# Idle rounds between the dependent steps of a closing that runs beside the scans of the next image

## The chip, the cores and the metric

The kernel runs on one core of one Trainium2 chip. The metric is the device time of one execution in microseconds (us); a lower number is better. Names of engines are those of the profile: PE is TensorE (PEld its weight loads), DVE is VectorE, ACT is ScalarE, POOL is GpSimd, SP is SyncE, which here only issues DMAs.

## The reference

Four images of 4096 tokens and 128 channels go through two layers, all in 32-bit floats.

```python
# layer 0: group norm, three selective scans (forward, backward, sliced order), out-projection, residual
x = x + conv(gn(x))
#   per order: silu(causal conv of the in-projection); delta = softplus(...)
#   h = h * exp(delta * A) + (delta * u) * B ;  y = sum_n h * C + D * u ;  y *= silu(z)
# layer 1: t are the tokens of x
t = t + attn(ln(t))
#   q = ring of cosines of (ln(t) + theta), 16 heads of 8;  softmax(q q^T / sqrt(8)) q
#   x1 = ln(x + ctx @ w_comb.T + b_comb)
#   z = cos(x1[:, :8]) * cos(ry);  out = ln(x1 + relu(z @ w1.T + b1) @ w2.T + b2)
t = t + experts(ln(t))
#   64 experts choose 8 tokens each by softmax(ln(t) @ gate.T); gelu network; scatter-add
```

## The kernel before

The work is issued in an order that the Python program writes out by hand (`tc.manual_schedule()`). Each engine takes its instructions in that order. The program mixes several streams of work. Every stream is a generator, and each `yield` in it ends one step.

**The main stream** is the attention loop of one image, `Attention.loop(b, beside)`. It has 1024 rounds (4 head groups, 8 blocks of 512 queries, 32 blocks of 128 keys). A round issues on PE the score matmuls of the next round (L917) and the value matmuls of this one (L931), and on ACT two exponentials of 128x1024 (`e<-s`, L922). At the end of a round `beside(i)` is called, which gives steps to the other streams. The four loops follow each other; before the rounds of a loop, SP issues the 16 loads of its `qT` and `v` (L896, L897).

**The scans** (`Scans.of_image`, the Pace `following`) of the next image run beside the loops of images 0, 1 and 2, 384 scan steps for an image. A scan step is two generator steps. In its first half it issues the loads of a later step (`delta`, `du`, on SP), the exponential of the next step (`exp`, ACT, L522) and, when its number modulo 4 (`turn`) is 1 or 2, the `y` sums of finished steps (PE, L570). In its second half it issues on DVE the scan (L538, 2.35 us) and two products (L529, L543, 1.2 us each); at `turn` 2 also `out` (L586), which reads `y` out of PSUM on DVE. Beside the loops the scans are paced so that they end near round 860.

**One PSUM bank** of the eight is left for everything beside the loop (`Bank(..., 1)`). `y` holds it from `turn` 1 to `turn` 2. Others ask for it with `bank.take`, which yields `PE` first; `beside` lets such a step go only when the bank is free and, as long as scans are left, only in a *slot*: a call of `beside` in which the scans issued an exponential but no sums (`turn` 3 and 0).

**The closing** (`Attention.after(b)`, the Pace `last`) is what remains of an image after its loop. It runs beside the next image's loop, at the front of it, one step in a round. For images 0 and 1 this is beside the scans of images 2 and 3 (loops 1 and 2); for image 2 it is beside the last loop, where no scans are left. Its parts:

- `shares()`: load the softmax totals (SP, L1001), take the reciprocal (DVE, L1003), store it (POOL, L1004).
- `first(g)` for 8 groups of 512 tokens: loads; `cT*part` (DVE, L1018); two halves of `co` (take, PE L1025; add on DVE L1028); a norm; store.
- `cosines()`: DVE and one sine on ACT.
- `second(g)` for 8 groups: transpose of z (`zt`), four `h` (PE L1059, evacuated on DVE L1062), four `fo` (PE L1069, added on DVE L1073), two norms with stores, transpose `xT` (L1090), `lg` (L1099).

`norm` makes statistics on DVE, a reciprocal root on POOL (`rstd_of`), yields, and scales on DVE (L831). `flow(pieces, 2, apart)` runs two groups at once, one step of each in turn; only one group at a time may hold the tile `h`, and the other one waits for it by yielding (`hidden`).

**The opening** of the next image (`opening(b + 1)`) starts when the scans of that image are done and the closing is done. What is left of closing or opening after round 1023 runs with no attention beside it:

```python
other = last if not last.done else opens if left == 0.0 else None
if other is None:
    return
slot = left == 0.0 or "exp" in scans.did and "sum" not in scans.did
if other.then is not PE or not bank.free:
    other.run(1.0)
    slot = slot and left > 0.0
if slot and other.then is PE and bank.free:
    other.run(1.0)
```

Of the kernel before, what the change touches and what calls it, by code (L numbers as in the profile page):

```python
# [669 lines left out]
class Attention:  # L670
# [3 lines left out]
    def __init__(self, tc, ctx, w, gate, cols, ident, bank, dram, t1, w_out, sums, sz, x):  # L674
        nc = self.nc = tc.nc
        gate_w, gate_b = gate
        self.tc, self.cols, self.ident, self.bank, self.dram, self.t1 = tc, cols, ident, bank, dram, t1
        self.w_out, self.sums, self.sz, self.x = w_out, sums, sz, x
        const = ctx.enter_context(tc.tile_pool(name="a_const", bufs=1))
        self.half_pi = column(nc, const, math.pi / 2.0, "a_half_pi")  # L680

        def rows(name, n):
            t = const.tile([P, n], F32, name=f"bc_{name}")
            nc.scalar.dma_start(out=t, in_=w[name].partition_broadcast(P))
            return t

        self.theta = rows("rx_theta", D)
        self.bc = {k: rows(k, C) for k in ("b_comb", "b2", "g1", "beta1", "g2", "beta2")}
        self.b1 = const.tile([P, 4], F32, name="b1")
        nc.scalar.dma_start(out=self.b1, in_=w["b1"].rearrange("(f p) -> p f", p=P))  # L690
        self.cos_ry = const.tile([D, 3], F32, name="cos_ry")
        nc.scalar.dma_start(out=self.cos_ry[:, 0:1], in_=w["ry_theta"].unsqueeze(1))
        cosine(nc, self.cos_ry[:, 2:3], self.cos_ry[:, 0:1], self.cos_ry[:, 1:2], self.half_pi)
        self.w_comb = const.tile([P, C], F32, name="w_comb")
        self.w1 = const.tile([D, FFN], F32, name="w1")
        self.w2 = const.tile([P, 4, C], F32, name="w2")

        self.mask = const.tile([P, 4], F32, name="mask")
        self.gate = const.tile([P, E], F32, name="gate")
        self.gate_b = const.tile([2 * E, 1], F32, name="gate_b")  # L700
        for k in range(2):
            nc.scalar.dma_start(out=self.gate_b[k * E : (k + 1) * E], in_=gate_b.unsqueeze(1))
        with tc.tile_pool(name="a_load", bufs=1) as load, tc.tile_pool(
            name="a_load_ps", bufs=2, space=PSUM
        ) as load_ps:
            raw = load.tile([P, C], F32, name="raw_comb")
            nc.sync.dma_start(out=raw, in_=w["w_comb"])
            ps = load_ps.tile([P, 512], F32, tag="ps", name="ps_comb")
            nc.tensor.transpose(ps[:, :C], raw, ident)
            nc.vector.tensor_copy(self.w_comb, ps[:, :C])  # L710
            raw = load.tile([P, 4, D], F32, name="raw_w1")
            nc.sync.dma_start(out=raw, in_=w["w1"].rearrange("(f p) d -> p f d", p=P))
            ps = load_ps.tile([P, 512], F32, tag="ps", name="ps_w1")
            for f in range(4):
                nc.tensor.transpose(ps[:D, f * P : (f + 1) * P], raw[:, f, :], ident)
            nc.vector.tensor_copy(self.w1, ps[:D])
            raw = load.tile([P, FFN], F32, name="raw_w2")
            nc.sync.dma_start(out=raw, in_=w["w2"])
            ps = load_ps.tile([P, 512], F32, tag="ps", name="ps_w2")
            for f in range(4):  # L720
                nc.tensor.transpose(ps[:, f * P : (f + 1) * P], raw[:, f * P : (f + 1) * P], ident)
            nc.vector.tensor_copy(self.w2.rearrange("p f c -> p (f c)"), ps)
            raw = load.tile([4, 4, 4, D], F32, name="raw_mask")
            nc.gpsimd.memset(raw, 0.0)
            nc.gpsimd.affine_select(
                out=raw, in_=raw, compare_op=ALU.not_equal, fill=1.0,
                base=0, pattern=[[0, 4], [-1, 4], [0, D]], channel_multiplier=1,
            )
            ps = load_ps.tile([P, 512], F32, tag="ps", name="ps_mask")
            nc.tensor.transpose(ps[:, :4], raw.rearrange("j i k d -> j (i k d)"), ident[:4, :4])  # L730
            nc.vector.tensor_copy(self.mask, ps[:, :4])
            raw = load.tile([E, C], F32, name="raw_gate")
            nc.scalar.dma_start(out=raw, in_=gate_w)
            ps = load_ps.tile([P, 512], F32, tag="ps", name="ps_gate")
            nc.tensor.transpose(ps[:, :E], raw, ident[:E, :E])
            nc.vector.tensor_copy(self.gate, ps[:, :E])
        self.small = ctx.enter_context(tc.tile_pool(name="a_small", bufs=2))
        self.u, self.q, self.v, self.context, self.total, self.t2 = {}, {}, {}, {}, {}, {}
        self.xn, self.logits, self.angled, self.whole, self.closed = {}, {}, {}, {}, {}

    def begin(self, loop):

# [25 lines left out]
    def tokens(self, b, g, angles):  # L768
# [47 lines left out]
        self.angled[b] += 1  # L816
        yield

    def norm(self, out, src, name):

        nc = self.nc
        stats = self.small.tile([P, 4, 6], F32, tag="ln_stats", name=f"st_{name}")
        mv = self.small.tile([P, 4, 2], F32, tag="ln_mv", name=f"mv_{name}")
        rstd = self.small.tile([P, 4], F32, tag="ln_rstd", name=f"rs_{name}")
        for i in range(4):
            nc.vector.bn_stats(stats[:, i, :], src[:, i, :])
            nc.vector.bn_aggr(mv[:, i, :], stats[:, i, :])
        rstd_of(nc, rstd, mv[:, :, 1], *self.cols)
        yield
        for i in range(4):  # L830
            nc.vector.tensor_scalar(  # L831
                out[:, i, :], src[:, i, :], mv[:, i, 0:1], rstd[:, i : i + 1], ALU.subtract, ALU.mult
            )
# [140 lines left out]
    def after(self, b, gs=range(L // QB), to=None):  # L974
# [21 lines left out]
        def shares():  # L996
            def rows(t):
                return t.rearrange("q h t -> (q h t)").rearrange("(p t) -> p t", p=P)

            t = self.piece([P, len(gs) * H * QB // P], "p0", name=f"sum_{b}_{gs[0]}")  # L1000
            nc.sync.dma_start(out=t, in_=rows(self.total[b][blocks]))  # L1001
            yield
            nc.vector.reciprocal(t, t)  # L1003
            nc.gpsimd.dma_start(out=rows(share), in_=t)  # L1004
            yield

        def first(g):
            cut = slice(g * 4, g * 4 + 4)
# [6 lines left out]
                out=part, in_=share[g - gs[0]].unsqueeze(1).to_broadcast([H, D, 512])  # L1015
            )
            yield
            nc.vector.tensor_mul(cT, cT, part)  # L1018
            yield
            yield  # L1020
            for half in range(2):
                ps = yield from self.bank.take(f"co_{b}_{g}_{half}")
                for k in range(2):
                    at = slice((2 * half + k) * P, (2 * half + k + 1) * P)
                    nc.tensor.matmul(ps[:, k * C : (k + 1) * C], cT[:, at], self.w_comb, start=True, stop=True)  # L1025
                yield
                u_h = flat(u[:, 2 * half : 2 * half + 2, :])
                nc.vector.tensor_add(u_h, u_h, ps[:, : 2 * C])  # L1028
                self.bank.leave()
# [8 lines left out]
        def second(g):  # L1038
# [11 lines left out]
            self.bank.leave()  # L1050
            yield
            yield
            while self.hidden == max(1, self.n - 1):
                yield
            self.hidden += 1
            h = self.one.tile([P, 4, 512], F32, tag="h", bufs=max(1, self.n - 1), name=f"h_{b}_{g}")
            for f in range(4):
                ps = yield from self.bank.take(f"h_{b}_{g}_{f}")
                nc.tensor.matmul(ps, self.w1[:, f * P : (f + 1) * P], zT, start=True, stop=True)  # L1059
                yield  # L1060
                if self.n == 2:
                    nc.vector.tensor_scalar(h[:, f, :], ps, self.b1[:, f : f + 1], 0.0, ALU.add, ALU.max)  # L1062
                else:
                    nc.scalar.activation(h[:, f, :], ps, AF.Relu, bias=self.b1[:, f : f + 1])
                self.bank.leave()
            for k in range(4):
                ps = yield from self.bank.take(f"fo_{b}_{g}_{k}")
                for f in range(4):
# [16 lines left out]
            nc.gpsimd.dma_start(out=self.xn[b][:, cut, :], in_=u)  # L1085
            yield
            yield
            ps = yield from self.bank.take(f"xT_{b}_{g}")
            for k in range(4):
                nc.tensor.transpose(ps[:, k * P : (k + 1) * P], u[:, k, :], self.ident)  # L1090
# [3 lines left out]
            self.bank.leave()  # L1094
            yield
            yield
            ps = yield from self.bank.take(f"lg_{b}_{g}")
            rows = slice(E, 2 * E) if to else slice(0, E)
            nc.tensor.matmul(ps[rows], self.gate, xT, start=True, stop=True)  # L1099
# [304 lines left out]
def tile_kernel(tc, ctx, x, in_proj_w, dirs, out_proj_w, attn, gate, weight1, weight2, out):  # L1404
# [47 lines left out]
    with tc.manual_schedule():  # L1452
        last = Pace()
        n = 3 * NC * NB
        for b in range(nb - 1):
            opens = Pace(block.opening(b + 1))

            def beside(i):

                left = 2.1 * (n + 1 - scans.steps.get(b + 1, 0))  # L1460
                scans.did.clear()
                following.run(min(1.3, max(0.5, left / max(1, 860 - i))))
                other = last if not last.done else opens if left == 0.0 else None
# [14 lines left out]
                following.run(0.5 if ready else 1.0)  # L1478
            last = Pace(block.after(b))
        following.rest()  # L1480

    scanning.close()
    experts = Experts(tc, ctx, ident, weight1, weight2, block, nb)
# [65 lines left out]
```

## Time and profile before

| what | value |
|---|---|
| median of 3 runs | 12901.4 us (12900.43 to 12902.03) |
| profiled execution, its own time | 12908.77 us |
| span of the profile | 12907.1 us |
| PE, ACT, DVE, POOL busy | 94%, 83%, 68%, 24% of the span |
| loop 1 (image 1, beside it closing of image 0, scans of image 2) | from 4991.9 us, 2597 us for its 1024 rounds |
| loop 2 (image 2, beside it closing of image 1, scans of image 3) | from 7593.0 us, 2580 us |

The profile is one execution. Busy time of PE is modelled, so a PE that is busy is not always a PE at its peak; a stretch in which it is idle is real. A round number in this document is counted in the trace: two exponentials `e` (L922) make one round, and the first of a loop is its round 0.

### The profile page before, as it was taken

The numbers are of one execution on the slowest core, as the hardware profiler recorded it, in microseconds if no ns is written. First come the engines' busy times: TensorE is split into PE (matmuls) and PEld (weight loads), VectorE is DVE, ScalarE is ACT, GpSimd is POOL, SyncE is SP. The second block draws the span as 40 slices with busy tenths as digits, with TensorE's granted clock in tenths as the row PEclk, the third lists the DMA queues.
The fourth block names the chain that finished last, engine by engine and source line by source line (L and its number), as shares of the span: only waits on it lengthen the run. The fifth ranks groups of instructions, "written<-read, shape, count | busy, mean of one in ns | idle before, by whom it ended". The sixth has DMA issues, their size and how long they took to land.

```text
span 12907.1 us, 215600 instructions
## 1 busy us (share of the span) xinstructions
PE 12125.7 (94%) x85447; PEld 3883.9 (30%) x85447; DVE 8730.9 (68%) x8912; ACT 10718.9 (83%) x10812; POOL 3129.4 (24%) x4007
## 2 busy tenths in 40 slices
PE   7888887599999999999999999999999999999996
PEld 3333333122222222333322222333222223333323
DVE  7999998788888877888887778888874211101112
ACT  5676766499999988999999889999998888888882
POOL 2324342232223222223232223232321000000000
PEclk9898988799999999999999999999999999999997
DMA  5666666555555455554554555545543100000004
GB/s 163 198 190 183 186 183 193 138 134 139 139 135 138 121 151 143 134 132 127 127 131 121 146 143 135 133 125 131 127 122 97 54 20 13 22 17 22 13 22 169
DMA packets 775661, 1553.29 MB, mean 120 GB/s; under 512 B 205198, under 2 KB 392134, under 8 KB 774390
## 3 DMA queue, kind: packets, MB, share of 16 engines
q1 hardware_dynamic: 590686, 1127.02, 33.7%
q0 software_dynamic: 142464, 302.77, 7.6%
q10 hardware_dynamic: 41496, 109.71, 3.3%
q8 instruction: 669, 10.96, 0.4%
q14 instruction: 346, 2.83, 0.1%
HBM read 1230.07 MB, written 308.81 MB: 119 GB/s over the span
## 4 chain that ended last, share of the span: by engine, by line
PE 80%; DVE 7%; ACT 5%; issue 4%; DMA 3%; SPq 1%; POOL 0%; ACTq 0%; DVEq 0%; POOLq 0%
PE s L917 36%; PE acc L931 29%; PE y L570 4%; PE cv L378 3%; DVE h L538 3%; PE sp L436 2%; PE fo L1069 1%; ACT e L922 1%; PE h L1059 1%; PE xd L392 1%; DVE dB L529 1%; DMA du<-d_du 1%; DMA w<-in_L_ffn_weight_dram 0%; DMA d_y<-o 0%; ACT e L424 0%
## 5 line engine op out<-in xcount | busy, mean ns | idle before, releaser
L922 ACT ACTIVATE e<-s 128x1024 f32<-128x1024 f32 x8192 | 7905.1, 1027 | 1107.0 <-PE s L917 940.4
L917 PE MATMUL s<-qm,qT 32*128 32x512 f32 x32768 | 5437.2, 642 | 112.5 <-DMA qT<-d_q 58.0
L931 PE MATMUL acc<-e,v 128*32 128x512 f32 x32768 | 4386.6, 607 | 24.4 <-ACT av L940 21.9
L917 PEld LDWEIGHTS s<-qm,qT 32*128 32x128 f32 x32768 | 1792.8, 183 | 3199.9 <-PE s L917 1408.6
L540 POOL COPY ends<-h 128x1 f32<-128x1 f32 x1152 | 1375.3, 1196 | 2875.1 <-DVE h L538 2866.0
L931 PEld LDWEIGHTS acc<-e,v 128*32 128x32 f32 x32768 | 646.9, 108 | 3162.8 <-issue 3021.4
L538 DVE TENSOR_TENSOR_SCAN h<-delta,ends,du 128x1024 f32<-128x1024 f32 x576 | 1351.6, 2347 | 196.6 <-ACT delta L522 162.2
L538 DVE TENSOR_TENSOR_SCAN h<-dA,ends,dB 128x1024 f32<-128x1024 f32 x576 | 1351.4, 2346 | 128.0 <-ACT dA L522 115.4
L529 DVE TENSOR_TENSOR dB<-du,B 128x1024 f32<-128x1024 f32 x768 | 929.6, 1210 | 657.1 <-PE y L570 595.0
L522 ACT ACTIVATE dA<-delta,A 128x1024 f32<-128x1024 f32 x768 | 888.0, 1156 | 147.3 <-DMA delta<-d_delta 146.3
L522 ACT ACTIVATE delta<-delta,A 128x1024 f32<-128x1024 f32 x768 | 887.1, 1155 | 137.6 <-PE y L570 127.8
L543 DVE TENSOR_TENSOR du<-h,C 128x1024 f32<-128x1024 f32 x768 | 936.5, 1219 | 0.1
L543 DVE TENSOR_TENSOR dB<-h,C 128x1024 f32<-128x1024 f32 x768 | 936.4, 1219 | 0.0
L529 DVE TENSOR_TENSOR du<-du,B 128x1024 f32<-128x1024 f32 x768 | 922.2, 1201 | 0.4 <-DMA B<-d_bc 0.3
L946 POOL DMA_DIRECT2D d_ctx<-av x512 | 259.9, 517 | 1248.2 <-ACT av L940 1242.7
L378 PE MATMUL cv<-xn,conv 128*128 128x512 f32 x1024 | 490.5, 632 | 33.0 <-DVE xn L313 17.3
L570 PE MATMUL y<-du,sel 128*32 128x256 f32 x6144 | 483.9, 387 | 17.3 <-DVE du L543 17.3
L570 PE MATMUL y<-dB,sel 128*32 128x256 f32 x6144 | 486.8, 389 | 4.3 <-DVE dB L543 3.4
L538 DVE TENSOR_TENSOR_SCAN h<-delta,du 128x1024 f32<-128x1024 f32 x192 | 438.7, 2285 | 45.8 <-ACT delta L522 37.8
L599 POOL DMA_DIRECT2D d_y<-o x512 | 328.5, 671 | 562.9 <-DVE o L586 430.8
L538 DVE TENSOR_TENSOR_SCAN h<-dA,dB 128x1024 f32<-128x1024 f32 x192 | 438.6, 2284 | 36.8 <-ACT dA L522 35.9
L564 POOL DMA_DIRECT2D d_du<-x_delta x272 | 154.4, 568 | 1132.2 <-DVE x_delta L563 1069.1
(255 smaller groups left out, 7643.6 us busy)
## 6 DMA issues: line engine op xcount, KB each, us to landing
delta<-d_delta SPq DMA_DIRECT2D x768, 512.0 KB
du<-d_du SPq DMA_DIRECT2D x576, 512.0 KB
du<-d_du ACTq DMA_DIRECT2D x192, 512.0 KB
d_u<-u POOLq DMA_DIRECT2D x48, 1024.0 KB, 5.7
B<-d_bc SPq DMA_DIRECT2D x96, 512.0 KB
C<-d_bc SPq DMA_DIRECT2D x96, 512.0 KB
d_delta<-r POOLq DMA_DIRECT2D x48, 1024.0 KB, 5.7
us<-d_u SPq DMA_DIRECT2D x384, 128.0 KB
```

Of the source, the lines that this page charges most:

```text
L378: nc.tensor.matmul(ps[:, cut], w["conv"][:, k, m * P : (m + 1) * P], reads(k, g), start=(k == 0), stop=(k == 3))
L522: nc.scalar.activation(tiles["delta", s], t, AF.Exp, scale=A)
L529: nc.vector.tensor_mul(tiles["du", s], du, spread[order, c, "B", j % 2])
L538: nc.vector.tensor_tensor_scan(h, dA, dB, first, ALU.mult, ALU.add)
L540: nc.gpsimd.tensor_copy(ends[order, c][:, at : at + 1], h[:, T - 1 :])
L543: nc.vector.tensor_mul(dB, h, spread[order, c, "C", j % 2])
L570: nc.tensor.matmul(y[32 * g : 32 * g + 32, : T // 4], self.sel[:, j // 2, :], hC[:, 256 * g : 256 * g + 256], start=(j == 0), stop=(j == 3),)
L599: nc.gpsimd.dma_start(out=to.rearrange("p (i j) -> p i j", i=SLICES)[:, :, at : at + n], in_=rows.rearrange("p (i j) -> p i j", i=SLICES),)
L917: nc.tensor.matmul(s_ps[:, k, :], qT[at : at + 32, kc * P : (kc + 1) * P], queries[j, qb][at : at + 32, :], start=True, stop=True,)
L922: nc.scalar.activation(e, s_ps, AF.Exp, scale=1.0 / math.sqrt(D))
L931: nc.tensor.matmul(accs[j, qb][32 * k : 32 * k + 32, :], v[:, kc, h * VW : h * VW + 32], es[i][k // 2][:, k % 2, :], start=(kc == 0), stop ...
L946: nc.gpsimd.dma_start(out=self.context[b][h * D : h * D + D, cut], in_=av[32 * k : 32 * k + D, :])
```

## The change

A method `settle(n)` is added to `Attention`; it yields `n * lag` times and issues nothing. `lag` is 2 in a round in which scans of the next image are left, and 0 otherwise (and after the three loops). Calls of it are put between a step of the closing and the next step that needs its result. No instruction is added, removed or altered; the order in which the closing's instructions stand among the others changes. `opening` and the norm in it call `settle` too, but only where `lag` is 0.

```diff
+        self.lag = 0
...
+    def settle(self, n=1):
+
+        for _ in range(n * self.lag):
+            yield
+
     def norm(self, out, src, name):
...
         rstd_of(nc, rstd, mv[:, :, 1], *self.cols)
         yield
+        yield from self.settle()
         for i in range(4):
             nc.vector.tensor_scalar(
...
             nc.sync.dma_start(out=t, in_=rows(self.total[b][blocks]))
             yield
+            yield from self.settle(3)
             nc.vector.reciprocal(t, t)
             nc.gpsimd.dma_start(out=rows(share), in_=t)
             yield
+            yield from self.settle(3)
...
                 out=part, in_=share[g - gs[0]].unsqueeze(1).to_broadcast([H, D, 512])
             )
             yield
+            yield from self.settle(2)
             nc.vector.tensor_mul(cT, cT, part)
             yield
             yield
+            yield from self.settle()
             for half in range(2):
                 ps = yield from self.bank.take(f"co_{b}_{g}_{half}")
...
             self.bank.leave()
             yield
             yield
+            yield from self.settle()
             while self.hidden == max(1, self.n - 1):
                 yield
...
                 self.bank.leave()
+            yield from self.settle()
             for k in range(4):
                 ps = yield from self.bank.take(f"fo_{b}_{g}_{k}")
...
             nc.gpsimd.dma_start(out=self.xn[b][:, cut, :], in_=u)
             yield
             yield
+            yield from self.settle()
             ps = yield from self.bank.take(f"xT_{b}_{g}")
...
             yield
             yield
+            yield from self.settle()
             ps = yield from self.bank.take(f"lg_{b}_{g}")
...
                 left = 2.1 * (n + 1 - scans.steps.get(b + 1, 0))
+                block.lag = 2 if left > 0.0 else 0
                 scans.did.clear()
...
         following.rest()
+    block.lag = 0
```

## The prediction

> **What bounds the kernel now.** I read the page's first three views, then the chain of work that ended last, then the windows, and then the idle stretches of PE in loops 1 and 2, because only there is `lag` above 0 while a closing runs.
>
> ```profile
> PE 12125.7 (94%) x85447; PEld 3883.9 (30%) x85447; DVE 8730.9 (68%) x8912; ACT 10718.9 (83%) x10812; POOL 3129.4 (24%) x4007
> ...
> PE   7888887599999999999999999999999999999996
> ...
> PE 80%; DVE 7%; ACT 5%; issue 4%; DMA 3%; SPq 1%; POOL 0%; ACTq 0%; DVEq 0%; POOLq 0%
> ```
>
> PE sets the pace: busy in nearly all of slices 9 to 39, and 80% of the chain. So a microsecond that PE stands idle in a loop is a microsecond of the kernel. The windows show where. I cut loop 1 into its front (two stretches), the long middle, the end of the closing (round 668, the last `lg`) and what follows, and loop 2's front likewise:
>
> ```profile
> core 0: us, PE busy (x) PEld busy (x) DVE busy (x) ACT busy (x) POOL busy (x), PEclk, DMA share, GB/s
> 4987.70:5165.00 177.30, 162.87 (x1240) 48.25 (x1240) 148.44 (x172) 147.76 (x155) 67.02 (x62) 0.96 0.66 178
> 5165.00:5331.00 166.00, 161.90 (x1274) 49.04 (x1270) 148.36 (x173) 153.40 (x159) 58.48 (x60) 0.98 0.50 133
> 5331.00:6601.00 1270.00, 1265.21 (x10038) 385.94 (x10030) 1063.39 (x1000) 1183.35 (x1229) 389.10 (x490) 1.00 0.51 130
> 6601.00:6769.00 168.00, 162.69 (x1290) 49.49 (x1290) 139.08 (x131) 150.28 (x157) 61.95 (x78) 0.98 0.50 125
> 7580.00:7772.00 192.00, 172.98 (x1304) 52.29 (x1300) 155.94 (x191) 154.48 (x161) 70.98 (x65) 0.93 0.61 168
> ```
>
> PE idles 14.4 us in the first stretch, 4.1 in the second, 4.8 in 1270 us of the middle, 5.3 at the end of the closing; and 19.0 in loop 2's front. The granted clock dips in the same stretches. The front is where `first` runs (`co` in rounds 10 to 93). PE's timeline says whom it waits for:
>
> ```profile
> 5012.90 2.08 PE L917 MATMUL s<-qm,qT 32*128 32x512 f32 x4 [6.18 <-ACT e L922]
> 5026.72 0.71 PE L1025 MATMUL co<-w_comb,cT 128*128 128x128 f32 x4 [1.73 <-DVE o L586]
> 5154.18 0.71 PE L1025 MATMUL co<-w_comb,cT 128*128 128x128 f32 x4 [3.88 <-DVE o L586]
> ...
> 6692.53 1.12 PE L1090 MATMUL xT<-ident,x1r 128*128 128x128 f32 x4 [5.04 <-DVE o L586]
> 7613.93 2.07 PE L917 MATMUL s<-qm,qT 32*128 32x512 f32 x4 [7.01 <-ACT e L922]
> 7632.22 1.22 PE L1025 MATMUL co<-w_comb,cT 128*128 128x128 f32 x4 [8.28 <-DVE o L586]
> ```
>
> The number in brackets is PE's idle time and what ended it. The common pattern: a closing's matmul needs the one bank, and `o` on DVE has not read the scans' `y` out of it. DVE is late, and its timeline says why:
>
> ```profile
> 5008.54 3.35 DVE L1003 RECIPROCAL sum<-sum 128x512 f32<-128x512 f32 x1 [17.97 <-DMA sum<-d_sum]
> 5011.81 2.25 DVE L538 TENSOR_TENSOR_SCAN h<-dA,ends,dB 128x1024 f32<-128x1024 f32 x1
> ...
> 6681.39 1.11 DVE L831 TENSOR_SCALAR x1r<-t,mv_x,rs_x 128x128 f32<-128x128 f32 x4 [1.44 <-POOL rs_x L45]
> ```
>
> The reciprocal stands 18.0 us in DVE's order with scans behind it (22.6 us in loop 2). In the rest of the front DVE is overfull: a `first(g)` takes 10.3 rounds and puts some 6.7 us on DVE (0.69 for `cT`, 0.84 for the adds, 0.69 for the bias, 1.8 for statistics, 2.7 for scale, g1, beta1, z) beside 4.1 scan steps of 4.8 us and 1.3 for `o` and products: 27.7 us of DVE for 10.3 rounds, which at the middle's 2.52 us are 26.0. In `second` a group spreads over 72 rounds and DVE has room.
>
> **What the Trainium skill says.** "PSUM — Partial Sum Buffer", Engine vs sequencer instructions: VectorE's queue is strictly first in, first out, and matmuls start in program order. The trace agrees: the scan at 5011.81 follows only when the reciprocal is through, and PE leaves `s` undone behind a waiting `co`. "TensorE: Matmul & The Clock Gate", Part 1: an idle PE falls to half clock and needs about 3.4 us of work to come back. The trace shows half clock in pieces of 3.4 us: 3.4 us from 5155.1, 6.8 from 6691.1, 10.2 from 7626.3, 6.8 from 7762.9. Half of what lies after the gap's end is lost as well.
>
> **The change, part by part.** No instruction changes, so each edit costs only by place. Rounds first. `first(g)` has 9 steps and gets 8 more (4+2 beside `cT`, 2 in the norm); `second(g)` has 32 and gets 12; `shares` gets 12. That is 12+64+96 = 172 rounds if nothing hides them. Slots hide much: the scans make 0.4 steps in a round, so two slots per ten rounds. Before, `first(g)` with its 2 takes filled one such cycle (10.3 rounds); with 17 steps it fills two (20), so the front ends near round 175 instead of 93. In `second(g)` its 8 takes for `h` and `fo` go at about one per cycle while the other group only spins; the 12 new steps replace spins, and a group stays near 70 rounds. Walking the steps through the rule of `beside` gives an end at 663 and 644 for the old order (trace: 668 and 635) and some 735 for the new one, in both loops. That is well before 860, where the opening starts. So the **added rounds cost nothing**: what covers them is the stretch from 668 to 860, in which `last` is idle. If that cover went, the slow rival below gives the price. The 172 rounds hold no DMA, and no bank is held across a `settle`, so nothing queues behind them.
>
> What each takes away (gap, plus half-clock loss after it):
> - `settle(3)` twice in `shares`: the reciprocal comes six rounds, about 16 us, later in DVE's order, so the 18.0 and 22.6 us waits mostly go, and two scan steps whose inputs are there (`dA` made at 4986.7 and 4998.5) run in that time. PE's gaps before the first `co`: 1.73 + 8.28 us and 2.2 us of half clock = **12.2**, between 0 and 12.2. The 6.18 and 7.01 us gaps before them stay: ACT waits there for `delta<-d_delta`, issued on SP at 5002.4 behind the 16 loads of `qT` and `v`, which the change doesn't move. With DVE free, ACT on `delta` is what is late next.
> - `first` at half the pace: gaps 0.90, 3.89, 1.17 (loop 1), 2.38, 2.16 (loop 2) = 10.5, half clock 1.7 + 3.4. Sum 15.6. DVE's load falls to 6.7 us in 20 rounds, as light as in `second`, whose 176 takes in both loops cost 3.6 us of gaps, 0.02 each; 32 takes leave 0.7. **14.9**, between 8 and 15.6.
> - `second` between zT and `h`, `h` and `fo`: gaps 0.64, 1.21, 0.54, 1.25 before `h`, which waits for DVE. I take half, **1.8**, between -2 and 3.6.
> - The last group runs alone, so its two norms, each with a 1.43 us wait for POOL, came within 15 us and `xT` found DVE behind: 5.04 and 1.99 us, half clock 2.7. Two rounds more at each of four places ease it, but `o` still has to come first: **5.7** of 9.7, between 0 and 9.7.
> - The sine's two table loads on ACT (gaps of 2.93 and 2.92 us) stay. The third closing and all openings run with `lag` 0: nothing.
>
> Sum 34.6 us, bounds 6 and 41. Against it I set 2 us for takes that fall on worse slots than before. From the profiled execution, 12908.8 us, that gives 12876; the median of the runs shown is 7.4 us lower, so **12869**.
>
> **Rivals.**
> - *The gaps move but do not close* (no change). `co` must still wait for `o` in the one bank, and slots come right after `turn` 2. For it: the bank isn't touched by the change. Against: the middle, with the same bank and slots and 0.4% idle. If it keeps the front's gaps but for the reciprocal, and half of that, the gain is 6 to 15 us: 12886 to 12896.
> - *Only the waits go, and the overfull front remains*: if two groups' bursts still coincide, half of the 34.6: 12884.
> - *The closing overruns the scans* (slower). If the slots aren't the limit in `second`, but each added step also draws a spin, 96 becomes 192, and with delays in the front the closing reaches some 900 rounds. Until round 874 nothing is lost: the opening, which starts at 860, ends at 1009 in loop 1 and 995 in loop 2, so 14 and 28 rounds are spare. At 905, 31 + 17 rounds of opening run after the loops with no attention beside. Image 0's opening, which also runs alone, took about 250 us, and an opening has some 149 steps (rounds 860 to 1009), so 1.7 us each: 82 us, less the 33 saved: 12950. For it: the second loop's margin rests on my count. Against: the count hits the old ends within 9 rounds.
> - That the change doesn't do what it says is excluded only where `lag` is 0: if the scans were done early it would act in fewer rounds. Scan step 384 comes at round 852 in all three loops, so it acts throughout.
>
> **How the numbers follow.** A measurement can tell about 0.2%, 26 us. The forecast, gains of 26 to 45 us, has 0.54; the two cases of smaller gains or none have 0.34, of which a few hundredths reach slightly past no change; the overrun, or a new stall of its size, has 0.12. The range runs from all bounds at their best and a little more, 12856, to a gain of a few us, 12897; it leaves out the slow case and a small part on each side.
>
> **What would show it.** In the profile after: the reciprocal's DVE wait under 5 us in both loops; no `co` with an idle time above 1 us; the two gaps of 6 to 7 us before `s` still there; last `co` near round 170 and last `lg` near 735; the front 128 rounds at 2.5 to 2.6 us each instead of 2.68 and 2.75. A last `lg` after 860, or openings that end after round 1023, would make the prediction wrong, and so would new gaps of PE on DVE between rounds 100 and 740.

## The result, and the profile after

The changed kernel takes 12872.9 us (median of 9 runs), the kernel before 12904.9 us in the same comparison: so the medians lie **32 us** apart. The ratio of the compared runs is 0.9972, 95% interval 0.9963 to 0.9981: **0.28% faster**, which is 36 us. The forecast was 12869 us. The span of the profile falls from 12907.1 to 12868.3 us. Of these 38.8 us, loop 1 gives 19.2 and loop 2 18.0; the rest are differences of a few us in parts whose order is unchanged (+2.4 before loop 0, +1.9 in loop 0, -4.8 in loop 3, -1.2 behind it).

The lines of the page after that answer to those of before:

```profile
PE 12115.7 (94%) x85447; PEld 3883.3 (30%) x85447; DVE 8731.8 (68%) x8912; ACT 10716.4 (83%) x10812; POOL 3005.4 (23%) x4007
...
PE   7888887599999999999999999999999999999996
...
PE 83%; ACT 5%; DVE 4%; issue 4%; DMA 3%; SPq 1%; POOL 0%; ACTq 0%; DVEq 0%; POOLq 0%
```

The counts of instructions are the same to the last one, and busy times nearly so, but for POOL's, which falls by 4%. The tenths of PE cannot show the change: a slice is 322 us long, and the gain in one loop is under 20. What moves is the chain: DVE's share falls from 7% to 4% and PE's rises from 80% to 83%, on a shorter span. Three hundredths of the span are ten times the gain, so the shares tell which engine ends the waits and not how much was gained. The windows answer the question where. They are the front of loop 1 in two stretches (rounds 0 to 63 and 64 to 127), its middle, the end of its closing, and the front of loop 2 in the same two stretches:

```profile
core 0: us, PE busy (x) PEld busy (x) DVE busy (x) ACT busy (x) POOL busy (x), PEclk, DMA share, GB/s
4992.10:5158.60 166.50, 160.03 (x1224) 46.78 (x1224) 133.94 (x125) 147.65 (x156) 48.26 (x55) 0.98 0.64 173
5158.60:5316.70 158.10, 158.10 (x1276) 47.22 (x1265) 145.46 (x159) 148.94 (x156) 63.64 (x59) 1.00 0.53 140
5316.70:6600.00 1283.30, 1278.09 (x10126) 389.63 (x10118) 1078.99 (x1030) 1196.85 (x1243) 367.25 (x496) 1.00 0.51 131
6600.00:6930.00 330.00, 328.94 (x2606) 100.62 (x2600) 280.78 (x267) 306.97 (x320) 123.85 (x155) 1.00 0.50 124
7574.00:7744.00 170.00, 160.36 (x1220) 46.79 (x1220) 133.29 (x124) 147.37 (x155) 47.96 (x54) 0.96 0.62 170
7744.00:7907.00 163.00, 162.73 (x1296) 48.19 (x1291) 149.22 (x147) 153.60 (x162) 60.12 (x60) 1.00 0.54 138
```

Before, the first 64 rounds of the two loops took 177.2 and 184.3 us; now 166.5 and 170.4. Rounds 64 to 127 took 166.3 and 167.5 us, now 158.1 and 159.2. In the second stretch PE hardly idles any more (0 and 0.3 us), and at the end of the closing it idles 1.1 us in 330. What is left is in the first stretch. PE's timeline of the kernel after, the stretches in which PE is idle and what ended them:

```profile
5016.20 2.08 PE L924 MATMUL s<-qm,qT 32*128 32x512 f32 x4 [4.91 <-ACT e L929]
...
5541.76 0.60 PE L1057 MATMUL zt<-ident,z 128*8 128x128 f32 x4 [1.38 <-DVE h L1074]
...
7601.17 2.08 PE L924 MATMUL s<-qm,qT 32*128 32x512 f32 x4 [8.57 <-ACT e L929]
```

No `co` and no `xT` stands here any more. The two gaps of round 6 do, as forecast (6.18 and 7.01 us before), and one of 1.38 us, in round 215, is new. DVE's timeline in the front of loop 1:

```profile
5016.40 1.23 DVE L529 TENSOR_TENSOR dB<-du,B 128x1024 f32<-128x1024 f32 x1 [9.75 <-DMA du<-d_du]
...
5023.92 3.34 DVE L1011 RECIPROCAL sum<-sum 128x512 f32<-128x512 f32 x1
```

The reciprocal waits for nothing now. In the same time DVE waits 9.75 us for `du`, the scans' own load: one wait took the place of the other.

### The profile page after: what moved, and what is told of

Same layout as the page of the kernel before. It is cut to its first block, busy times and chain, and to the rows that moved or that the text cites. A ratio compares the mean times of both kernels' runs of the same rounds, so it can differ in the third digit from the quotient of the medians.

```text
span 12868.3 us, 215630 instructions
## 1 busy us (share of the span) xinstructions
PE 12115.7 (94%) x85447; PEld 3883.3 (30%) x85447; DVE 8731.8 (68%) x8912; ACT 10716.4 (83%) x10812; POOL 3005.4 (23%) x4007
## 4 chain that ended last, share of the span: by engine, by line
PE 83%; ACT 5%; DVE 4%; issue 4%; DMA 3%; SPq 1%; POOL 0%; ACTq 0%; DVEq 0%; POOLq 0%
PE s L924 37%; PE acc L938 30%; PE y L570 5%; PE cv L378 3%; PE sp L436 3%; DVE h L538 2%; PE fo L1082 1%; PE xd L392 1%; ACT e L929 1%; PE h L1071 1%; DMA w<-in_L_ffn_weight_dram 1%; DMA delta<-d_delta 0%; SPq L889 0%; ACT ln L429 0%; ACT e L424 0%
## 5 line engine op out<-in xcount | busy, mean ns | idle before, releaser
L540 POOL COPY ends<-h 128x1 f32<-128x1 f32 x1152 | 1248.2, 1086 | 2939.8 <-DVE h L538 2929.1
```

The source lines that it names most:

```text
L540: nc.gpsimd.tensor_copy(ends[order, c][:, at : at + 1], h[:, T - 1 :])
```

## The experiments

The kernels of the twelve experiments ran in three groups, each compared with runs of the kernel before on the same chip. Times scatter by several us and the intervals of neighbouring kernels overlap, so a difference of less than some 10 us between two of these kernels can't be told from the times. A second reading from each profile helps, though a profile is one execution: the time of rounds 0 to 831 in loops 1 and 2 together, and the idle stretches of PE over 0.5 us in that part, added up by the matmul that ended them ("round 6" are those before `s` or `acc` in rounds 0 to 8 or just ahead of them; "front" those before `co`, and before `y` in the front; "second" those before `zt`, `h`, `xT`, `lg` and before `y` later; gaps before `s` in later rounds, as at the sine's table loads, stand in no column), and the time at half clock in us. Experiments 7 and 11 have their numbers in their own paragraphs.

| kernel | ratio to before (95% interval) | rounds 0-831, us | round 6 | front | second | half clock |
|---|---|---|---|---|---|---|
| before | 1 | 4235.1 | 14.7 | 20.5 | 10.7 | 61.4 |
| the change | 0.9972 (0.9963-0.9981) | 4195.5 | 15.5 | 0 | 1.4 | 27.3 |
| shares only | 0.9999 (0.9990-1.0007) | 4228.9 | 15.6 | 15.6 | 12.6 | 41.0 |
| first only | 0.9983 (0.9975-0.9991) | 4207.7 | 14.1 | 0 | 9.3 | 37.5 |
| second only | 0.9992 (0.9984-1.0000) | 4217.0 | 13.2 | 21.8 | 1.2 | 47.8 |
| yields at the ends | 1.0004 (0.9996-1.0012) | 4235.3 | 14.8 | 13.6 | 12.5 | 51.2 |
| only before cT | 0.9988 (0.9980-0.9996) | 4215.2 | 13.9 | 0.8 | 13.8 | 41.0 |
| only before co, norm | 0.9990 (0.9982-0.9999) | 4225.4 | 15.4 | 1.3 | 19.1 | 68.3 |
| first and second | 0.9978 (0.9970-0.9986) | 4199.3 | 12.5 | 0 | 0 | 27.3 |
| later loads, no waits | 0.9988 (0.9982-0.9995) | 4221.8 | 2.1 | 21.7 | 10.3 | 51.2 |
| the change, later loads | 0.9955 (0.9942-0.9967) | 4177.0 | 2.1 | 0 | 0.9 | 13.7 |
| first, second, later loads | 0.9966 (0.9952-0.9979) | 4193.6 | 1.5 | 0 | 0 | 23.9 |

**1. The waits in shares alone.** Edit: of the change's calls of `settle`, only these two stay.

```diff
             yield
+            yield from self.settle(3)
             nc.vector.reciprocal(t, t)
             nc.gpsimd.dma_start(out=rows(share), in_=t)
             yield
+            yield from self.settle(3)
```

> Only the two waits in shares() are kept; first and second run as before. Theory (the sum of the prediction): the reciprocal no longer stands in DVE's order, the gaps of 1.73 and 8.28 us before the first co go, the front stays overfull: 12 us faster than before, 0.1%, first co near round 25, last co near 115. Rival 1 (the reciprocal's wait is what made DVE late in the whole front, so with it gone the front catches up by itself): 25 us or more faster, no co with an idle time above 1 us. Rival 2 (the reciprocal's wait was covered by the wait for delta): within 4 us of before.

Measured: no gain (12905.8 us against 12905.3). The first 64 rounds did shorten, by 9.7 and 9.5 us, and the gap of 8.28 us went. But loop 1 lost it again in the next 64 rounds (178.6 us in place of 166.3). DVE's timeline of this kernel there, and PE's:

```profile
5244.04 0.69 DVE L1027 TENSOR_TENSOR cT<-cT,part 128x512 f32<-128x512 f32 x1 [10.55 <-DMA part<-d_share]
```

```profile
5249.63 1.08 PE L570 MATMUL y<-dB,sel 128*32 128x256 f32 x8 [8.78 <-DVE x L1037]
```

`cT*part`, one step behind its loads, stood 10.55 us in DVE's order because `part` landed late; behind it stood the add that reads `co` out of the bank, and PE waited 8.78 us with `y`. Before, the same product waited at most 3.5 us in this front: it was the same danger, with a luckier place. The theory's 12 us did not come. The number is that of rival 2 (within 4 us of before), and its reason comes up again in experiments 2, 9 and 12; but it is not the whole story, since the first gaps did close here and others opened behind them. Taking the reciprocal's wait away alone is not a gain that one can keep.

**2. The waits in first alone.** Edit: only the three calls in `first(g)` (one of them in its norm).

> Only the waits in first(g), its norm included, are kept. Theory: DVE's load in the front falls from 27.7 us in 10.3 rounds to the level of second; the gaps before co behind rounds 50 go, the one at round 10 (8.28 us in loop 2) stays or moves as the reciprocal still waits 18 to 23 us: 15 us faster than before, front ends near round 180. Rival 1 (the reciprocal is the cause of all): within 5 us of before. Rival 2 (first alone is the whole gain): 30 us faster.

Measured: 23.1 us faster (12882.3 against 12905.3). Every gap of the front is gone, also those that the prediction had put down to the reciprocal, although it waits as before; the two longest waits of DVE in the first 200 rounds of loop 2, total, times and longest in us:

```profile
DVE dB L529 <- PE y L570: 26.9, 11, 5.7
DVE sum L1010 <- DMA sum<-d_sum: 23.1, 1, 23.1
```

So the 23.1 us wait does not hurt by itself. The likely reason is that DVE had little it could do then, with `delta` and `du` late too, and that the wait hurt only when the first `co` came before DVE had caught up; here the first `co` comes 12 rounds later than before. Experiments 9 and 12 test this. The gaps of `second` stay (9.3 us).

**3. The waits in second alone.** Edit: only the six calls in `second(g)`, two of them in norms.

> Only the waits in second(g), its two norms included, are kept. Theory: the gaps before xT of the last group (5.04 and 1.99 us) shrink and those before h go; the front is as before: 7 us faster, 0.06%, last lg within 20 rounds of before, since the new steps replace spins. Rival (added steps come on top of the spins): last lg above round 720; the time moves little even so. The front's gaps before co are expected unchanged under both.

Measured: 8.7 us faster (12896.6 against 12905.3; the interval reaches to no change), near the 7 us expected. The gaps of `second` fall from 10.7 to 1.2 us and those of the front are as before. The last `lg` comes at rounds 655 and 617 (668 and 635 before): the new steps cost no rounds at all here, because they stand where the other group only spun.

**4. As many yields, at the ends of the parts.** This asks whether the pace or the distance between dependent steps counts.

```diff
             nc.gpsimd.dma_start(out=rows(share), in_=t)
             yield
+            yield from self.settle(6)
...
             nc.gpsimd.dma_start(out=mid[:, cut, :], in_=u)
             yield
+            yield from self.settle(4)
...
             self.closed[b] += 1
             yield
+            yield from self.settle(6)
```

> As many added yields as in the change, but all at the end of a part: 12 behind shares, 8 behind each first(g), 12 behind each second(g), none between a step and the one that needs its result. Theory (the front's gaps come from the pace, the others from dependent steps that stand too close): the front gains its 15 us, the reciprocal keeps its 18 to 23 us wait, the gaps before xT of the last group stay: 15 us faster. Rival 1 (only the separation of dependent steps matters): within 5 us of before. Rival 2 (only the number of rounds matters): as fast as the change, 32 us faster.

Measured: no gain (12910.8 against 12905.3), which is the side of rival 1 (the distance counts, not the number of rounds). A group of `first` takes 18 rounds here in place of 10, but a third of the front's gaps went at most (13.6 us of 20.5), and new ones came in `second`. DVE's timeline in the front of loop 2 shows what the pace does not mend, and PE's what came of it:

```profile
7784.50 0.41 DVE L1036 TENSOR_TENSOR x<-x,co 128x256 f32<-128x256 f32 x1
...
7788.79 1.11 DVE L838 TENSOR_SCALAR x<-x,mv_x,rs_x 128x128 f32<-128x128 f32 x4 [1.43 <-POOL rs_x L45]
...
7796.00 0.41 DVE L1036 TENSOR_TENSOR x<-x,co 128x256 f32<-128x256 f32 x1
```

```profile
7796.47 1.08 PE L570 MATMUL y<-dB,sel 128*32 128x256 f32 x8 [3.69 <-DVE x L1036]
```

Between 7784.5 and 7791.5 the add, the norm with its wait for POOL, the scale and g1, beta1 follow each other without a scan between them, however long the pause behind them is. The next group's add comes late behind that, and PE waits 3.69 us. It may not be the burst alone: at 7769.96 us, ahead of these lines, `cT*part` had stood 6.05 us for `part`. Experiment 11 was made to tell the two apart.

**5 and 6. The waits of first, divided.** One kernel keeps `settle(2)` before `cT*part` alone, the other one keeps `settle()` before `co` and in the norm.

> One wait alone: settle(2), four yields, between the loads of first(g) and the product cT*part. Theory after the first four runs (the front's loss is DVE standing in order for the load of part, which lands late when the front's transfers collide): at least 15 us faster than before, no wait of DVE for part above 1 us, no gap before co or y above 2 us, although the reciprocal keeps its wait of 17 to 23 us. Rival (it is co that stands too close behind cT and behind the scans' o, or the norm's scale behind POOL): under 8 us faster, gaps before co stay.

> The counterpart: of the waits in first(g) only those before co and in the norm are kept, the four yields before cT*part are not. Theory (part's load): under 8 us faster than before, DVE waits for part again for 4 us or more in a loop, gaps of PE before co or y remain. Rival (distance of co and of the norm): 15 us faster or more.

Measured: 17.6 and 12.6 us faster (12893.7 and 12898.8 against 12911.4). Each half alone takes the front's gaps almost wholly (0.8 and 1.3 us are left); in experiment 6 `part` still costs DVE one wait of some 4.5 us in each loop, with a gap of 0.7 us at most. All that experiment 5's theory expected came (no wait for `part` above 0.5 us, 17.6 us gained), but experiment 6, with 12.6 us and the front's gaps gone too, lies between its theory and its rival. So the load of `part` is not the only cause: no single pair of steps makes the front's loss. Against experiment 2 both lose in `second`, where their gaps are 13.8 and 19.1 us (before `h` and `xT`, 5.5 and 6.6 us before the last group's `xT` in experiment 5). A likely reading, not tested by itself, is that the front's length shifts how the steps of `second` fall among the scans, and that without waits of its own `second` is at the mercy of that.

**7. lag 6 in place of 2.** The edit is the number.

> lag 6 in place of 2, so that the closing overruns the scans. By the count of steps the closings end near rounds 970 and 975 and the openings 85 to 100 rounds after each loop's end. Slow rival of the prediction (1.7 us for each opening step with no attention beside): 2 x 90 x 1.7 = 300 us slower than the change, near 13175 us. If steps beside nothing cost only what DVE and DMA need: near 100 us slower. If the closing does not overrun: within 10 us of the change.

Measured: 13168.7 us, 2.0% slower than before (1.0201, 1.0187 to 1.0215). The last `lg` comes at rounds 990 and 945, and from the last round of loop 1 to the first of loop 2 there are 272.5 us in place of 4.2. PE's timeline in that hole:

```profile
7772.37 1.08 PE L570 MATMUL y<-dB,sel 128*32 128x256 f32 x8 [13.62 <-DVE o L586]
...
7822.51 5.28 PE L924 MATMUL s<-qm,qT 32*128 32x512 f32 x16 [44.99 <-DVE qm L913]
```

PE waits for the opening's chain, and at last 45 us for loop 2's first `qm`, whose `qT` is loaded from what the opening has just stored. Behind loop 2 the opening's `out` matmuls run among the first rounds of loop 3, where PE then waits 48 us before a `co`; 64 rounds take 227.7 us there in place of 152.6. The price of the prediction's slow rival is right in sum, in part by luck: it had the same loss behind each of the two loops, where the trace, against that of the change, has 248 us more in loop 1, 24 us less in loop 2 and 76 us more behind them. In rounds 0 to 831 (4150.9 us, shorter than with `lag` 2, as much of the closing comes later) no gap before `co`, `y`, `h`, `xT` or `lg` is over 0.5 us, so the front's gain does not hang on the one value of `lag`.

**8. The change with later loads of qT and v.** This goes for what the change left.

```diff
-        for g in range(NT // 4):
+        def bring(g):
             nc.sync.dma_start(out=qT[:, g * 512 : (g + 1) * 512], ...)
             nc.sync.dma_start(out=v[:, g * 4 : g * 4 + 4, :], ...)
+        for g in range(3):
+            bring(g)
...
             beside(i)
+            if i % 3 == 1 and 3 + i // 3 < NT // 4:
+                bring(3 + i // 3)
```

> The change, and of the 16 loads of qT and v only six are issued ahead of a loop; the other ten follow at rounds 1, 4, 7, 10 and 13, behind that round's scan loads. Theory (the gaps of 4.9 and 8.6 us before s in round 6 come from delta's load standing behind those 16 on SP): both fall under 2 us, ACT's wait for delta under 1 us, 10 to 18 us faster than the change, near 12858 us. Rival 1 (the transfers share the same DMA engines, so delta lands as late): within 4 us of the change. Rival 2 (late chunks are late for the rounds that need them): new gaps before s or acc between rounds 10 and 28, slower than the change.

Measured: 12851.7 us, 0.45% faster than before (0.9955, 0.9942 to 0.9967). This is **the fastest version**. The windows of the first 64 rounds of loops 1 and 2, widened by a few us:

```profile
core 0: us, PE busy (x) PEld busy (x) DVE busy (x) ACT busy (x) POOL busy (x), PEclk, DMA share, GB/s
4996.00:5159.10 163.10, 161.44 (x1260) 47.53 (x1256) 137.35 (x127) 151.50 (x159) 50.04 (x56) 1.00 0.70 182
7573.00:7734.40 161.40, 160.60 (x1256) 47.41 (x1256) 137.31 (x127) 150.81 (x158) 53.53 (x56) 1.00 0.71 184
```

PE idles 1.7 and 0.8 us there and keeps its full clock. ACT's wait for `delta` falls from 6.2 to 0.6 us in loop 1. So rival 1 is wrong, but that does not make SP's order the only reason. For loop 1, SP's issue of `delta` and the window around it, first of the change, then of this kernel:

```profile
5005.75 0.55 SPq L508 DMA_DIRECT2D delta<-d_delta  x1
5004.00:5008.00 4.00, 4.00 (x38) 1.28 (x32) 2.35 (x1) 3.87 (x5) 0.18 (x1) 1.00 1.04 402
...
5006.91 0.56 SPq L508 DMA_DIRECT2D delta<-d_delta  x1
5004.00:5008.00 4.00, 4.00 (x36) 1.17 (x32) 0.00 (x0) 2.75 (x4) 0.00 (x0) 1.00 0.49 166
```

Counted from the start of the loop (4996.3 and 5000.3 us), `delta` is issued after 9.5 us in the change and after 6.6 us here. ACT begins to work on it 8.3 and 5.6 us after the issue. In the change the DMA engines are full when it is issued (a share of 1.04), here half of their time is free (0.49). So of the 5.5 us that `delta` comes earlier, about half is its place in SP's order, and about half is the shorter time behind the issue, which goes with the emptier engines. The edit changes both at once.

**9. First and second, without shares.**

> The change without the two waits in shares(). Theory after eight runs (the reciprocal's wait of 17 to 23 us costs nothing as long as the first co comes late enough, since DVE would wait for delta in that time anyway; the gain is that of first, 23 us, and of second, 9 us): 32 us faster than before, as fast as the change, although the reciprocal waits 17 us or more; no gap before co, xT or h above 1.5 us in loops 1 and 2. Rival (the three parts add, as the prediction had it): 12 us slower than the change, 20 us faster than before.

Measured: 27.7 us faster (12879.3 against 12907.1; 0.9978). Its interval holds both expectations. By the trace it is 3.8 us behind the change in rounds 0 to 831, with no gap in front or second, and the reciprocal waits 17.6 and 22.4 us. By that trace the waits in shares are worth about 4 us here; the times cannot tell it from nothing.

**10. Later loads in the kernel before, without any added wait.**

> The kernel before, with only the later loads of qT and v (six ahead of the loop, ten at rounds 1 to 13) and no added waits. Theory (two separate causes: the loads on SP make the gaps before s in round 6, the closing's own order makes those before co and xT): the gaps of 6.2 and 7.0 us go, 15 to 20 us faster than before; gaps before co behind round 20 and before xT of the last group stay. Rival 1 (the burst of loads is behind the front's gaps too): 30 us or more faster, no gap before co above 1 us. Rival 2 (without the waits DVE becomes late at once and eats the gain): under 8 us.

Measured: 15.5 to 17 us faster (12890.1; 0.9988). The gaps of round 6 go (14.7 to 2.1 us), those of front and second stay; PE's timeline in loop 2:

```profile
7620.70 1.22 PE L1031 MATMUL co<-w_comb,cT 128*128 128x128 f32 x4 [9.64 <-DVE o L586]
```

Two causes, then, and two remedies whose gains add up within the noise: 17 us and 32 us alone, 59.7 us together in experiment 8 (43 to 75 us by its interval), and in rounds 0 to 831 13.2 and 39.6 us alone, 58.1 us together.

**11. The yields at the ends, without the wait for part.**

```diff
-            nc.vector.tensor_mul(cT, cT, part)
+            nc.vector.tensor_mul(cT, cT, cT)
```

> The kernel with the added yields at the ends of the parts, in which cT is multiplied by itself and not by part: part is still loaded, but DVE no longer waits for it (the division by the softmax total is left out). Theory (with the pace alone, the front's loss is the wait for part, 14 to 17 us a loop, in DVE's order): the waits go, the front's gaps before y and co above 1.5 us go, 15 us faster than the kernel with the yields at the ends, near 12893 us. Rival (adds and norm in one burst on DVE make o late whatever part does): within 5 us of it, the gaps before y at rounds 74 and 113 stay.

Measured: 12901.0 us, a ratio of 0.9996 (0.9988 to 1.0004) to before, where the kernel with `part` had 1.0004 in another group. The experiment failed to remove what it was after: the product now waits nearly as long for `cT` itself. Its waits in loop 1's front:

```profile
DVE cT L1026 <- DMA cT<-d_ctx: 15.0, 3, 9.9
```

The gaps before `y` at rounds 74 and 113 stay, as the rival had it, at 1.4 to 2.0 us (1.4 to 3.7 us in experiment 4). How much of experiment 4's front is due to late loads and how much to DVE's bursts stays open. That the product waits up to 10 us there for its loads in general, and not for `part` alone, is shown.

**12. First, second and later loads, without shares.**

> The later loads of qT and v together with the waits in first and second, without those in shares. Theory: as fast as the change with later loads, near 12852 us, 0.45% faster than before, since the totals now land early too and the reciprocal hardly waits. Rival (with the loads out of the way the reciprocal's wait is no longer covered by that for delta): gaps of PE in rounds 5 to 15, 5 to 12 us slower than that.

Measured: 12864.7 us (0.9966), the rival's side, though its interval overlaps that of experiment 8: 16.6 us more than experiment 8 in rounds 0 to 831. PE's timeline in loop 2:

```profile
7607.30 1.22 PE L928 MATMUL s<-qm,qT 32*128 32x512 f32 x4 [2.86 <-ACT e L933]
7621.59 1.85 PE L928 MATMUL s<-qm,qT 32*128 32x512 f32 x4 [2.22 <-ACT e L933]
```

These gaps, at rounds 11 and 15, are not in experiment 8 (loop 1 has 1.14 and 1.48 us in the same rounds). The totals land earlier than before, but the reciprocal still waits 10.8 and 14.2 us, and now `delta` no longer covers for it. So, by the traces, the waits in shares gain nothing alone, little within the change, and count once the other delay of the front is gone.

## Why the prediction was right, point by point

- **The path.** "A microsecond that PE stands idle in a loop is a microsecond of the kernel" held: front and second lost 29.8 us of gaps and half clock fell by 34 us, half of which is lost work, some of it inside the gaps; rounds 0 to 831 became 39.6 us shorter. The sum of the prediction was 34.6 less 2.
- **The rounds.** Forecast: the front ends near 175, the closing near 735, in both loops. Measured: last `co` at 177 and 186, last `lg` at 755 and 765. The count was 20 to 30 rounds short, harmless with 860 as the bound; the openings end at 1009 and 995 as before. Experiment 7 shows that the bound is there and what it costs to cross it.
- **The gaps that stay.** 6.18 and 7.01 us before `s` in round 6: still 4.91 and 8.57. The reason given, `delta` behind 16 loads on SP, is borne out by experiment 8, where those loads delay it both in SP's order and on the full DMA engines. "What is late next" was the scans' loads: `du` (9.75 us on DVE) besides `delta`. The prediction let two scan steps run in the time set free because their `dA` was made; it overlooked that the second one's products would have to wait for `du`.
- **The term of shares, 12.2 us: mis-attributed.** The two gaps went, but not because the reciprocal's wait went. Experiment 2 removes them with that wait in place, and experiment 1 takes the wait away and gains nothing. The step that failed was to give a gap to the one longest wait ahead of it: more than one edit can close it alone (experiments 1 and 2 both do), and the terms for shares and first did not simply add.
- **The term of first, 14.9 us: the sum of both was right, the reason half.** First alone brought 23 us, most of the 27.1 of the two terms. "First at half the pace", an average load of DVE, is not enough: experiment 4 has the pace and no gain. By the comparison with the change, which has as many rounds, what counts is that DVE gets to the scans between a closing's load, product, add and norm.
- **The total was closer than its terms.** Forecast 34.6 less 2, measured 32 by the medians. That is luck in part: shares were put at 12.2 us and gave 0 to 4, first at 14.9 and gave 23, and the two misses cancel.
- **The last group, 5.7 of 9.7 us, and h, 1.8 of 3.6: both too cautious.** No gap before `xT` or `h` is left; the objection that `o` still has to come first carried no weight once DVE was not late. One gap of 1.38 us before `zt` is new, within the 2 us set aside, though it is of the kind that the prediction had named as a sign against it (PE on DVE between rounds 100 and 740).
- **The rivals.** "The gaps move but do not close" is refuted by the front's zero; the change of the bank was not needed. It is what happens to the partial edits, though: experiments 1, 5 and 6 closed gaps in one place and met others later. The overrun did not come with `lag` 2; with `lag` 6 it cost 296 us against the change (289 us with each taken against its own runs of the kernel before), where 300 was expected from the prediction's price of a step; the sum fits better than its parts.
- **The clock.** The Trainium skill states that an idle PE falls to half clock ("TensorE: Matmul & The Clock Gate", Part 1), and the traces agree: with fewer gaps the time at half clock fell from 61.4 to 27.3 us.

## What to carry to other kernels

Where several streams share in-order engines, an instruction that waits can hold up all that stands behind it, so put rounds between a load or a result and the step that needs it; here the same number of rounds behind the whole part brought nothing. Check first that the stretch into which the stream grows is really free, and where it ends. Remove one wait of a crowded front at a time only to learn: here one remedy alone was worth nothing until another delay was gone, and issuing ten loads later on SP was worth about half as much as all the added rounds.

## What the hardware showed beyond that

The same load can keep an engine waiting for very different times. DVE waited at most 3.5 us for `part` in the fronts of the kernel before, and 10.55 us in experiment 1, for the same tile and size. That load was issued at 5233.88 us, and from 5232 to 5244 us the DMA engines were busy to 96, 99 and 89% in stretches of 4 us: it shared them with other loads of the front.

Half clock needed less than the one idle window of about 3.4 us that the Trainium skill names ("TensorE: Matmul & The Clock Gate", Part 1). An idle stretch of 2.38 us (before `co` in round 60 of loop 2, kernel before) and one of 2.69 us (before `s` in round 196 of loop 2, the change) were each met by 6.8 us at half clock, while stretches of 2.16 and 1.99 us in the kernel before had none. The length of one stretch does not decide it alone: the one of 1.65 us before `s` in round 187 of loop 1 had none in the change, and in experiment 8 it was followed, 1.7 us after its end, by 6.8 us. What decides it stays open.
